# Layer 0 of a four-layer graph network: place 4 of a part hands on five far targets instead of four, and ScalarE scales three of them there

## The chip, the cores and the metric

The kernel runs on one core of a Trainium2 chip, in one launch. The core has a matrix engine (TensorE, PE in the profile; its weight loads are listed as PEld), a vector engine (VectorE, DVE), an engine for activation functions (ScalarE, ACT), a general engine (GpSimd, POOL) and a queue that issues transfers (SyncE, SP). Each works through its own list of instructions in order and waits for the others by semaphores. The metric is the device time of one execution in microseconds (us); before the change it is 3322.97 us, the median of three executions (3311.76 to 3326.16).

## What is computed

Four layers work on `x`, 64 graphs of 256 nodes with 256 features each, and on `adj`, 64 matrices of 256x256. The change is in layer 0 alone. That layer is a recurrence over the nodes: step `i` replaces row `i` of the state `h`, and the row is worked out from a weighted sum over all rows, among them those that earlier steps have replaced.

```python
def step(h, i):
    x = jnp.take(h_e, i, axis=1)
    row = jnp.take(norm_adjT, i, axis=1)
    x_par = jnp.einsum('bj,bjd->bd', row, h)
    iou = x @ W_ioux.T + b_ioux + x_par @ W_iouh.T + b_iouh
    r, z = jnp.split(iou, 2, axis=1)
    r, z = (jax.nn.sigmoid(r), jax.nn.sigmoid(z))
    hc = jnp.tanh(x @ W_coux.T + b_coux + x_par * r @ W_couh.T + b_couh)
    h_new = z * x_par + (1.0 - z) * hc
    h = jax.lax.dynamic_update_slice(h, h_new[:, None, :], (0, i, 0))
    return (h, None)
```

So there are 256 steps, each of which needs the one before. Layers 1 to 3 (two graph convolutions and two kinds of attention, each with a residual and a layer norm) follow; no line of them is touched.

## The kernel before

All of layer 0 is in `_recurrence`. A step works on one 128x128 tile: 64 graphs times two halves of the features on the 128 partitions, 128 features along them. The steps are grouped into parts of `U = 8`; the *place* of step `n` in its part is `p = n % 8`. The order of instructions on every engine is the order in which the program writes them (`tc.manual_schedule()`), so no scheduler moves anything.

The chain of a step is this. The sum `xp` (L878) is turned on TensorE (L612) and copied by ScalarE (`xpT`, L614). TensorE makes the gates from it (`h_part`, L605). ScalarE takes the sigmoid (`rs`, L836), TensorE turns it (L838), VectorE multiplies (`rT`, L840), TensorE makes the candidate (L605), ScalarE takes the tanh in place (L873, its tile is called `rc`). VectorE makes `zcc` (L875) and the next step's `xp` (L878). While that runs TensorE also adds the input's share for the next step (`x_part`, L597), and behind it stands the turn of the next `xp` (L612).

What a new state adds to the sums of later steps is spread over several engines. `sums[a]` (tile `ACC`) holds the sums of part `a`, and step `n` has state `j = n - 1` in hand. Its targets `m` are the steps from `n + 1` up to the end of the next part.

- The *near* targets go into the list `pushes` and are added by VectorE one at a time (L630, `ACC[m] += keep * S`). At places 1 to 7 the one for step `n + 1` comes first, then five more, and up to two more after the instruction that makes `v` (L865, its tile is called `keep`). What remains is added in the next step.
- The last `FAR[p]` targets are the *far* ones. They are remembered in `far` and dealt with in the next step, in one batch: `scale_far` lets ScalarE scale the first `begun` of them into the tile `far` (L667, directly behind `xpT` and ahead of `rs`), GpSimd scales the rest in one instruction (L672) and adds all of them to `ACC` in one (L676). The tile `far` has one buffer.
- GpSimd's list in a step is: `ready` (L817, the sum of step `n + 1` times its factor, which needs the first push), L672, L676, at places 3 and 4 the additions of `early_sb` (L830), at places 6 and 7 those of `late_sb` (L888). Now and then a piece of a table `An` (L479) or of a tile `xA` (L333) is cut at the end of a step, both from tiles that a transfer fills.

With `FAR = (3, 5, 5, 5, 4, 4, 3, 4)`, place 3 of part `a` hands on targets 8a+11 to 8a+15, and they are added at place 4. At place 4 the new state 8a+3 has eleven targets, 8a+5 to 8a+15: seven near ones, to 8a+11, and four far ones, 8a+12 to 8a+15, which are added at place 5. VectorE's list at place 4 is therefore: `keep` and `hs` (the state, L646 and L648), six pushes, `rT`, L858, `v` (L865), the seventh push (8a+11), `zcc`, `xp`.

SyncE issues the transfers: new states into a ring `Hw` (L656), from which at places 0 to 3 TensorE makes the `late` sums (L521), and loads and stores for the `early` sums, the tables and the sums `Us`.

Of the kernel before, what the change touches and what calls it, by code (L numbers as in the profile page):

```python
# [70 lines left out]
def _recurrence(tc, ident, Hd, x, adj, W_ioux, b_ioux, W_iouh, b_iouh, W_coux, b_coux, W_couh, b_couh, wide, then):  # L71
# [27 lines left out]
    XB = 4  # L99
    NG = B // 4  # L100
    HB = B // 2
    FAR = (3, 5, 5, 5, 4, 4, 3, 4)

    with ExitStack() as ctx:
        const = ctx.enter_context(tc.tile_pool(name="r_const", bufs=1))
# [140 lines left out]
        def next_of(queue, n):  # L246
            if queue:
                queue.pop(0)(n)
# [371 lines left out]
        def cell(j, m, count=1):  # L620

            a, u = divmod(m, U)
            k, i = divmod(m, T)
            return sums[a][:, u:u + count, :], tables[k]["S"][:, LAG + j - k * T, i:i + count]
# [37 lines left out]
        def scale_far(j, hs, first, count, begun):  # L662

            acc, s = cell(j, first, count)
            tmp = work.tile([P, 5, P], F32, tag="far", name=f"far_{j}_{first}", bufs=1)
            for e in range(begun):
                nc.scalar.activation(tmp[:, e, :], hs, AF.Copy, scale=s[:, e:e + 1])  # L667

            def finish():
                if begun < count:  # L670
                    shape = [P, count - begun, P]
                    nc.gpsimd.tensor_mul(  # L672
                        tmp[:, begun:count, :], hs.unsqueeze(1).to_broadcast(shape),
                        s[:, begun:count].unsqueeze(2).to_broadcast(shape),
                    )
                nc.gpsimd.tensor_add(acc, acc, tmp[:, 0:count, :])  # L676

            return finish
# [89 lines left out]
        for now in range(N):  # L768
            n = now
            k, i = divmod(n, T)  # L770
            p = n % U
# [1 line left out]

            xpT = flip(xp, "xpT", n)
            next_of(copies, n)
            add_far = far and scale_far(*far, min(2, far[-1]))

            far = []
            if n:
# [4 lines left out]
                to = list(range(n + 1, end))  # L784
                near = to[:len(to) - max(0, min(FAR[p], len(to) - 2))]
                far = (n - 1, hs, to[len(near)], len(to) - len(near)) if near != to else []
# [686 lines left out]
def kernel(ctx: ExitStack, tc: tile.TileContext, ins, out):  # L1473
# [14 lines left out]
    def load_layers(load):  # L1488
        weights.extend(
            _load_layers(nc, wide, load, ins["L1_gnn_W"], ins["L1_gnn_b"], l2, l3)  # L1490
        )

    _recurrence(
        tc, ident, Hd, x, adj,
        *(ins["L0_gnn_" + n] for n in (
# [44 lines left out]
```

## Time and profile before

| what | number |
|---|---|
| median of three executions | 3322.97 us (3311.76 to 3326.16) |
| the profiled execution: its time / the span of its instructions | 3317.71 us / 3315.6 us |
| layer 0's steps in the profiled execution | about 138 to 1475 us of the span |
| busy in 138 to 1475 us: PE / DVE / POOL / ACT | 1210.94 / 979.48 / 910.10 / 806.28 us |
| DMA engines' busy share in that stretch | 0.66 |
| one push, L630, 128x128 | 343 ns, 1592 of them |
| one scaling on ScalarE, L667, 128x128 | 397 ns, 503 of them |
| L672 on GpSimd, 128x128 / 128x256 / 128x384 | 399 / 613 / 826 ns |
| L676 on GpSimd, 128x384 / 128x512 / 128x640 | 1000 / 1273 / 1550 ns |
| `early_sb`'s addition L830, 128x512 | 1273 ns |
| usual length of a step at places 3, 4, 5, 6 (from the end of one `xp` to the next, median) | 4.89, 5.23, 5.11, 4.63 us |

The durations are means of groups of one shape between 200 and 1400 us, but for L630 and L667, which are given with their counts in the whole run. A time in a list of instructions counts from the start of the span. In square brackets behind an instruction stands how long its engine was idle before it, and which instruction let it go on. ACT's and DVE's instructions overlap with their neighbours a little, so that a row's length is more than what it adds to a queue: two scalings in a row are listed as 0.69 us together, not 0.79. The lengths of steps are medians over the 32 parts, read off the starts and ends of the instructions L878.

### The profile page before, as it was taken

To read this page: it belongs to the slowest core of one execution; us is meant where nothing else is said; L and a number is where in the kernel's file an instruction comes from. 1 tells how busy PE (TensorE), PEld (TensorE's weight loads), DVE (VectorE), ACT (ScalarE), POOL (GpSimd) and SP (SyncE) were. 2 spreads that over 40 slices of the span, in tenths; PEclk is the share of its full clock that TensorE was granted. 3 is DMA by queue.
4 is the path that set the end of the run, shared out by engine and by line. 5 is a ranking of instruction groups with operands and counts; after the bars stand their busy time and mean duration, and the time that the engine had idled before them with its cause. 6 is when DMAs were issued, how large, how long until landed. Compare 5 with 4: busy or idle time off the path is not lost.

```text
span 3315.6 us, 80692 instructions
## 1 busy us (share of the span) xinstructions
PE 3072.3 (93%) x28332; PEld 2274.1 (69%) x28332; DVE 2592.5 (78%) x7391; ACT 1982.0 (60%) x5193; POOL 1873.1 (56%) x2226
## 2 busy tenths in 40 slices
PE   5799998998888998976999999999999999999997
PEld 4566665555555555545888888888888888888885
DVE  3477777766666777765888888888888888888885
ACT  0266665655555665644666666666666666666664
POOL 2376776766566877843555555555555555555543
PEclk8999999999899999998999999999999999999998
DMA  9856676788777575334333333333333333333310
GB/s 300 244 163 157 170 196 153 179 195 210 188 192 168 150 186 146 100 77 94 76 77 79 77 77 79 79 77 75 80 76 79 77 78 77 78 77 77 77 43 20
DMA packets 807151, 398.35 MB, mean 120 GB/s; under 512 B 525148, under 2 KB 773096, under 8 KB 801512
## 3 DMA queue, kind: packets, MB, share of 16 engines
q1 hardware_dynamic: 789048, 376.25, 46.4%
q10 hardware_dynamic: 17696, 16.91, 1.5%
q8 instruction: 227, 3.72, 0.5%
q14 instruction: 180, 1.47, 0.1%
HBM read 274.34 MB, written 99.61 MB: 113 GB/s over the span
## 4 chain that ended last, share of the span: by engine, by line
PE 77%; DMA 8%; POOL 5%; DVE 4%; issue 3%; SPq 2%; ACT 1%; POOLq 0%; ACTq 0%; DVEq 0%
PE mm L1017 14%; PE rc L605 6%; PE rc L597 4%; PE s L1243 4%; PE mm_3v L1017 4%; PE mm_2f L1017 4%; PE late L521 3%; PE mm_2v L1017 3%; PE mm_3f L1017 3%; PE mm_t L1017 3%; PE mm_g L1017 3%; PE mm_2w L1017 3%; PE mm_2s L1017 3%; PE o L1278 3%; POOL ACC L676 2%
## 5 line engine op out<-in xcount | busy, mean ns | idle before, releaser
L1255 POOL TENSOR_TENSOR p3s<-p 128x256 f32<-128x256 f32 x512 | 358.7, 732 | 271.9 <-ACT p L1253 271.6
L1017 PE MATMUL mm<-xT,weights 128*128 128x256 f32 x2048 | 484.2, 385 | 2.7 <-ACT xT L1133 2.7
L630 DVE SCALAR_TENSOR_TENSOR ACC<-keep,S,ACC 128x128 f32<-128x128 f32 x1592 | 447.6, 343 | 39.3 <-POOL ACC L676 24.3
L676 POOL TENSOR_TENSOR ACC<-ACC,far 128x640 f32<-128x640 f32 (+2 forms) x312 | 404.3, 1296 | 69.5 <-ACT far L667 30.6
L1017 PEld LDWEIGHTS mm<-xT,weights 128*128 128x128 f32 x2048 | 386.4, 191 | 80.2 <-ACT xT L1133 28.8
L1252 DVE TENSOR_TENSOR p<-s,neg 128x512 f32<-128x512 f32 x512 | 317.7, 683 | 85.6 <-PE s L1243 85.6
L973 ACT ACTIVATE y<-y,shift,rstd 128x256 f32<-128x256 f32 x512 | 279.7, 596 | 158.1 <-DVE shift L971 157.9
L1253 ACT ACTIVATE p<-p 128x512 f32<-128x512 f32 x512 | 307.2, 629 | 3.5 <-DVE p L1252 3.0
L817 POOL TENSOR_TENSOR ready<-ACC,dinv 128x128 f32<-128x128 f32 x255 | 101.8, 399 | 312.1 <-DVE ACC L630 309.5
L597 PE MATMUL rc<-WxT,xqT 128*64 128x256 f32 x2048 | 275.7, 390 | 1.8 <-issue 1.8
L965 POOL TENSOR_TENSOR rstd<-rstd,mhalf 128x2 f32<-128x2 f32 x256 | 173.5, 696 | 134.9 <-DVE rstd L964 133.1
L672 POOL TENSOR_TENSOR far<-hs,S 128x384 f32<-128x384 f32 (+1 forms) x310 | 222.0, 716 | 4.7
L1292 DVE RECIPROCAL rT<-o 128x256 f32<-128x256 f32 x128 | 223.8, 1748 | 0.0
L961 DVE BATCH_NORM_STATS2 st<-y 128x6 f32<-128x256 f32 x512 | 209.6, 409 | 12.5 <-POOL y L1154 9.7
L605 PE MATMUL rc<-WhT,rT 128*64 128x128 f32 x2048 | 172.6, 290 | 37.3 <-DVE rT L840 33.6
L1165 ACT ACTIVATE qk<-mm,weights 128x256 f32<-128x256 f32 x256 | 107.3, 470 | 161.4 <-PE mm L1017 159.5
L521 PE MATMUL late<-Hw,An 64*32 64x256 f32 x3840 | 166.4, 400 | 40.3 <-DMA Hw<-hs 18.5
L1154 POOL TENSOR_TENSOR y<-y,g 128x512 f32<-128x512 f32 x64 | 81.1, 1267 | 215.3 <-ACT g L1151 179.3
L605 PEld LDWEIGHTS rc<-WhT,rT 128*64 128x64 f32 x2048 | 109.2, 138 | 133.9 <-DVE rT L840 110.9
L605 PE MATMUL rc<-WhT,xpT 128*64 128x128 f32 x2048 | 170.0, 287 | 17.6 <-ACT xpT L614 17.5
L614 ACT COPY xpT<-xpT_ps 128x128 f32<-128x128 f32 x256 | 68.0, 265 | 195.3 <-PE xpT_ps L612 195.0
L597 PEld LDWEIGHTS rc<-WxT,xqT 128*64 128x64 f32 x2048 | 140.6, 140 | 56.3 <-ACT rc L873 10.2
(169 smaller groups left out, 7375.0 us busy)
## 6 DMA issues: line engine op xcount, KB each, us to landing
xX<-in_x_dram ACTq DMA_DIRECT2D x16, 1024.0 KB
Us<-xu SPq DMA_DIRECT2D x64, 256.0 KB
xq<-in_x_dram SPq DMA_DIRECT2D x64, 256.0 KB
ACC<-Us SPq DMA_DIRECT2D x32, 512.0 KB
Es<-eu SPq DMA_DIRECT2D x64, 256.0 KB
early_sb<-Es SPq DMA_DIRECT2D x32, 512.0 KB
xin<-in_x_dram SPq DMA_DIRECT2D x64, 256.0 KB
ad<-in_adj_dram SPq DMA_DIRECT2D x64, 256.0 KB
```

The lines of the kernel that those rows point to most:

```text
L521: nc.tensor.matmul(pb[g][q * T:(q + 1) * T, e, :], An[rows, b].rearrange("p u s -> p (u s)"), Hw[rows, b, :], start=True, stop=True,)
L597: nc.tensor.matmul(G[o * B:(o + 1) * B], xqT[a, i // 2][:, i % 2, kc, h * B:(h + 1) * B], WxT[:, kc, o, gates], start=False, stop=False, s ...
L605: nc.tensor.matmul(G[o * B:(o + 1) * B], hT[:, kc * B:(kc + 1) * B], WhT[:, kc, o, g], start=False, stop=(kc == 1), skip_group_check=True,)
L630: nc.vector.scalar_tensor_tensor(acc[:, 0, :], keep[:, j % 2, :], s, acc[:, 0, :], ALU.mult, ALU.add)
L672: nc.gpsimd.tensor_mul(tmp[:, begun:count, :], hs.unsqueeze(1).to_broadcast(shape), s[:, begun:count].unsqueeze(2).to_broadcast(shape),)
L676: nc.gpsimd.tensor_add(acc, acc, tmp[:, 0:count, :])
L973: nc.scalar.activation(y[:, c, :], y[:, c, :], AF.Identity, bias=shift[:, c:c + 1], scale=rstd[:, c:c + 1],)
L1017: nc.tensor.matmul(pm[:, c, :], lhsT[:, k, c * P:(c + 1) * P], rhs[:, k, :], start=(k == 0), stop=(k == 1),)
L1252: nc.vector.tensor_add(p, s_ps[i], self.neg3)
L1253: nc.scalar.activation(p, p, AF.Exp, scale=ISQ)
L1255: nc.gpsimd.tensor_add(both, p[:, 0, :], p[:, 1, :])
L1292: nc.vector.reciprocal(rT, o_ps[:, 1, :])
```

## The change

```diff
-    FAR = (3, 5, 5, 5, 4, 4, 3, 4)
+    FAR = (3, 5, 5, 5, 5, 4, 3, 4)
...
-            add_far = far and scale_far(*far, min(2, far[-1]))
+            add_far = far and scale_far(*far, min(3 if p == 4 else 2, far[-1]))
```

`FAR[4]` goes from four to five. Target 8a+11 of state 8a+3 is no longer VectorE's seventh push at place 4; it is one of a batch of five (8a+11 to 8a+15) that is scaled and added at place 5. The second line works at place 4 on the batch that place 3 handed on: ScalarE scales three of those five, and GpSimd two.

The lists of the engines change as follows, in 31 of the 32 parts (in the last part fewer targets are left, and nothing changes).

| engine, place | before | after |
|---|---|---|
| DVE, place 4 | six pushes, then one behind `v` | six pushes, none behind `v` |
| ACT, place 4 | two scalings between `xpT` and `rs` | three |
| POOL, place 4 | L672 128x384, L676 128x640 | L672 128x256, L676 128x640 |
| POOL, place 5 | L672 128x256, L676 128x512 | L672 128x384, L676 128x640 |

The counts of instructions on PE, ACT, POOL and SP by kind are otherwise as before, apart from the 31 pushes that VectorE loses and the 31 scalings that ScalarE gains; no transfer is added, removed or moved in its queue.

## The prediction

> **What bounds the kernel now.** I read the page's costliest groups first, then VectorE's waits in layer 0, then one step at place 4 in order of time on each engine. Two groups of the page carry the work that the change shifts:
>
> ```profile
> L630 DVE SCALAR_TENSOR_TENSOR ACC<-keep,S,ACC 128x128 f32<-128x128 f32 x1592 | 447.6, 343 | 39.3 <-POOL ACC L676 24.3
> L676 POOL TENSOR_TENSOR ACC<-ACC,far 128x640 f32<-128x640 f32 (+2 forms) x312 | 404.3, 1296 | 69.5 <-ACT far L667 30.6
> ```
>
> The end of the first line matters: before pushes VectorE sat idle for 39.3 us, 24.3 of them until a far addition on GpSimd was done. VectorE's waits between 140 and 1475 us (who waits for whom, us in total, times, longest) say in how many places:
>
> ```profile
> DVE zcc L875 <- ACT rc L873: 123.0, 132, 7.1
> DVE ACC L630 <- POOL ACC L676: 24.3, 30, 1.2
> DVE keep L865 <- POOL ready L817: 13.2, 2, 8.7
> ```
>
> Thirty times, about once a part. Where it is shows in order of time. VectorE in step 100 (place 4 of part 12):
>
> ```profile
> 647.87 0.36 DVE L865 SCALAR_TENSOR_TENSOR keep<-keep,Sd,ready 128x128 f32<-128x128 f32 x1
> 648.99 0.35 DVE L630 SCALAR_TENSOR_TENSOR ACC<-keep,S,ACC 128x128 f32<-128x128 f32 x1 [0.76 <-POOL ACC L676]
> 649.26 0.28 DVE L875 TENSOR_TENSOR zcc<-zc,rc 128x128 f32<-128x128 f32 x1
> 649.57 0.35 DVE L878 SCALAR_TENSOR_TENSOR xp<-zcc,Sd,keep 128x128 f32<-128x128 f32 x1
> ```
>
> GpSimd in the same step:
>
> ```profile
> 646.15 0.40 POOL L817 TENSOR_TENSOR ready<-ACC,dinv 128x128 f32<-128x128 f32 x1 [0.85 <-DVE ACC L630]
> 646.51 0.83 POOL L672 TENSOR_TENSOR far<-hs,S 128x384 f32<-128x384 f32 x1
> 647.41 1.54 POOL L676 TENSOR_TENSOR ACC<-ACC,far 128x640 f32<-128x640 f32 x1
> 648.91 1.27 POOL L830 TENSOR_TENSOR ACC<-ACC,early_sb 128x512 f32<-128x512 f32 x1
> ```
>
> And ScalarE:
>
> ```profile
> 645.27 0.69 ACT L667 ACTIVATE far<-hs,S 128x128 f32<-128x128 f32 x2
> 646.34 0.28 ACT L836 ACTIVATE rs<-rc 128x128 f32<-128x128 f32 x1 [0.37 <-PE rc L605]
> 648.38 0.26 ACT L873 ACTIVATE rc<-rc 128x128 f32<-128x128 f32 x1 [0.31 <-PE rc L605]
> ```
>
> The seventh push writes target 8a+11. GpSimd's addition from 647.41 covers 8a+11 to 8a+15 and stands ahead of that push in the program, so the push waits until 648.99. The tanh had ended at 648.64. `zcc` could have followed it directly; it starts at 649.26, since it stands behind the push. Its sum is not read before step 8a+11, seven steps later, yet it holds up the recurrence. At other places pushes that stand behind `v` (place 3, for one) write targets which the running addition doesn't cover, and no row shows them waiting.
>
> How much of that the chain feels is read on TensorE. From tanh's start to the next turn of `xp` (L612) it is 1.60 us here (648.38 to 649.98). Two steps later, where nothing waits:
>
> ```profile
> 658.71 0.26 ACT L873 ACTIVATE rc<-rc 128x128 f32<-128x128 f32 x1 [0.43 <-PE rc L605]
> ...
> 659.84 0.33 PE L612 MATMUL xpT_ps<-ident,xp 128*128 128x128 f32 x1
> ```
>
> That is 1.13 us, and TensorE has no gap there, as it comes straight from `x_part`. So 0.47 us of the 0.59 us by which `zcc` is late is lost; the next 0.12 us would be covered by `x_part`.
>
> [...] For prices I use the trace[...], and L676 goes from 1273 to 1550 ns; [...] and the second scaling adds 0.69 less 0.40, or 0.29 us.
>
> **The change, part by part.** *The push goes (31 times).* I formed the time from tanh's start to the next L612, less 1.124 us (the finer value of 1.13), at place 4 of each of the first 31 parts: 17 parts show 0.47 or 0.48 us (sum 8.07), four 0.37 to 0.43 (1.56), two 0.58 (1.15), five 0.83 to 0.95 (parts 7, 25, 27, 28 and 29, where GpSimd comes late from two additions of early sums or a cut; 4.62), one 0.12, and two nothing. Sum 15.5 us. The push's own 0.34 us is in that sum and gives nothing more. What is late next is TensorE's `x_part`; it is why I take 15.5 us and not the 24.3 us of the waits.
>
> *The third scaling on ScalarE (31 times 0.29 us).* It stands between `xpT` and `rs`, which is on the chain. `rs` starts 0.37 us after the second scaling ends, waiting for TensorE; as instructions may overlap by 0.11 us, 0.48 us are free. I read the same room in each part: 0.47 us or more in 16 of 31, 0.33 to 0.34 in the others, against 0.29 needed. TensorE hides it everywhere, in those 15 parts with 0.04 us to spare only. Cost 0; if that cover failed it would be 31 x 0.29 = 9.1 us at most, less where `rT` waits for VectorE's pushes anyway.
>
> *GpSimd at place 4.* L672 is 0.21 us shorter (826 to 613 ns). It lets L676 and L830 end earlier by that. Now nothing on the chain waits for L676, so no gain.
>
> *GpSimd at place 5.* L672 takes 0.21 and L676 0.28 us more, together 0.49 us. L676 now covers 8a+11, so it must wait for the sixth push of place 5: in part 12 the scaling would be done about 0.1 us before that push is, a wait of some 0.1 us. Behind it stand `ready` of place 6 (L817) and, through the one buffer of `far`, ScalarE's scalings at place 6. Before `ready` at place 6 GpSimd idles 1.0 us or more in 28 of 31 parts, and in the other three `ready` ends 1.9 us or more before L865 starts. Cost 0; bound 31 x 0.6 = 18.6 us if no cover existed.
>
> *`ready` at place 5.* The steps come earlier by up to 0.95 us, GpSimd's list of place 4 by 0.21 only. The tightest parts (22, 25, 26, 28, 29) have 0.52, 0.87, 0.52, 0.84 and 0.84 us between the end of `ready` and L865; each keeps 0.1 to 0.15 us. Cost 0, bound 0.2 us each.
>
> *Waits on transfers.* In 14 parts place 0 is longer than its usual 4.70 us by 0.9 to 6.6 us, 46 us in all, as TensorE's late sums wait for `Hw` and other transfers; in parts 13 and 17 `ready` at place 5 waits behind a cut that waits for `raw` (4.5 and 8.7 us). SyncE's queue works there without a pause from place 4 on, so a step that arrives earlier can just wait longer. Gains ahead of such a wait: 5.6 us before the long places 0, 0.9 in parts 13 and 17, 1.0 before waits in parts 24 and 27: 7.5 us at risk. The trace can't show how much is swallowed. Bounds: 0 and 7.5 us, and below nothing (waits that shrink) as executions differ by 14 us anyway. I take 3 us, less than half, because part of those transfers wait themselves for states or sums that come earlier too.
>
> Sum: 15.5 - 3 = 12.5 us; the profiled execution's 3317.7 us becomes 3305.2. The median lies 5.3 us above that execution, which gives 3310.5; I say 3310.
>
> **The rivals.** *Kept in full.* Transfers follow the steps and their waits shrink a little: 3323 - 15.5 - 4 = 3303. For it: late parts (27 to 30, 3.2 us) have hardly a transfer wait, and SyncE waited often for VectorE. Against: the busy DMA share of 0.66.
> *Swallowed.* All 7.5 us are lost, and `rs` or `ready` take some 3 us more: gain 5 us, 3318. For it: long unbroken stretches of SyncE's queue between 490 and 512 us. Against: the parts without such waits hold 8 us by themselves.
> *Slower: `ready` behind the transfer of `raw`.* Place: place 4 or 5 of parts with a cut L479. GpSimd stands in order; when `raw` isn't there, `ready`, `v` and all else wait, which cost 3.6 and 7.9 us beyond a usual step twice in this trace. If earlier steps shift the queue so that four more parts are caught at 6 us each, and the transfers swallow half the gain, it is 3323 + 24 - 8 = 3339. It decides from three such parts on (18 us against the 15.5). Against: the change adds no transfer.
>
> **How the numbers follow.** Forecast (3310) 0.45, kept in full 0.28, swallowed 0.17, slower 0.10. A measurement of this kernel can tell about 0.5%, 16.6 us, from no change. Faster by more than that, below 3306.4: the rival kept in full nearly whole (0.26) and the lower two fifths of the forecast (0.18), 0.44. Slower by more than that, over 3339.6: some half of the last rival and a little spread, 0.06. The rest, 0.50, is within. Range 3297 to 3326: down to the full gain with its spread of 6 us, up past the swallowed case with executions' spread; it leaves out the slower rival and small tails.
>
> **What would show it.** In the changed trace VectorE's wait for L676 (24.3 us, 30 times) should be gone, `zcc` at place 4 start about 0.03 us behind the tanh's end, and place 4 be shorter by about 0.5 us. `rs` at place 4 should still wait for TensorE. L676 at place 5 should show a short wait for VectorE's push. I am wrong if `rs` is released by a scaling, if `ready` at place 5 or 6 ends L865's waits in many parts, or if places 0 to 3 grow by what place 4 loses.

## The result, and the profile after

| | before | after |
|---|---|---|
| median of nine executions | 3317.74 us (3311.76 to 3326.16) | 3307.10 us (3298.50 to 3317.09) |
| the profiled execution: time / span | 3317.71 / 3315.6 us | 3312.54 / 3310.8 us |
| before the first turn L612 / all steps / behind the last turn | 136.17 / 1336.41 / 1843.03 us | 140.53 / 1326.65 / 1843.63 us |

The ratio of after to before is 0.9964 [0.9947, 0.9982] (it is not the quotient of the medians, which is 0.9968); the medians lie 10.6 us apart. Nine executions put the kernel before at 3317.74 us; the 3322.97 that the prediction started from were the first three of them. Forecast were 3310 us, by a gain of 12.5. The gain is under the 0.5% (16.6 us) that the prediction took to be the least one could tell from no change; with nine executions of each the interval nevertheless ends below 1.

The span fell by 4.8 us only. The steps themselves took 9.8 us less, and 4.4 us came on before the first step, where no line of the change is at work. A single execution of each says little about the total: between two profiles of the changed kernel place 0 alone differs by 8.7 us (227.7 below and 236.4 when it was run again). Where time moved is therefore read from the rows of a place, and how much it is worth from the medians.

VectorE's waits between 140 and 1475 us, after (who waits for whom, us in total, times, longest):

```profile
DVE zcc L875 <- ACT rc L873: 138.6, 164, 7.8
...
DVE ACC L630 <- POOL ACC L888: 16.4, 7, 4.0
DVE keep L865 <- POOL ready L817: 14.2, 2, 9.7
```

The line of the pushes with L676, 24.3 us in 30 waits before, is gone. `zcc` waits for the tanh 164 times instead of 132, which is as it should be, since the tanh is on the chain and the push was not. L888's 16.4 us were 10.3 in four waits before; GpSimd's addition of `late_sb`, for which they wait, waits for a transfer itself. The two waits for `ready` are the same two parts as before. The page's groups say the same (31 pushes fewer, L630's idle time 20.8 us instead of 39.3, of which 16.4 behind L888):

```profile
L630 DVE SCALAR_TENSOR_TENSOR ACC<-keep,S,ACC 128x128 f32<-128x128 f32 x1561 | 436.8, 343 | 20.8 <-POOL ACC L888 16.4
L676 POOL TENSOR_TENSOR ACC<-ACC,far 128x640 f32<-128x640 f32 (+2 forms) x312 | 412.8, 1323 | 67.5 <-ACT far L667 27.6
```

In order of time, VectorE in step 100 (place 4 of part 12), after:

```profile
650.92 0.36 DVE L865 SCALAR_TENSOR_TENSOR keep<-keep,Sd,ready 128x128 f32<-128x128 f32 x1
651.73 0.29 DVE L875 TENSOR_TENSOR zcc<-zc,rc 128x128 f32<-128x128 f32 x1 [0.45 <-ACT rc L873]
652.05 0.35 DVE L878 SCALAR_TENSOR_TENSOR xp<-zcc,Sd,keep 128x128 f32<-128x128 f32 x1
```

ScalarE in the same step:

```profile
648.32 0.98 ACT L667 ACTIVATE far<-hs,S 128x128 f32<-128x128 f32 x3
649.38 0.28 ACT L836 ACTIVATE rs<-rc 128x128 f32<-128x128 f32 x1
...
651.43 0.26 ACT L873 ACTIVATE rc<-rc 128x128 f32<-128x128 f32 x1 [0.31 <-PE rc L605]
```

The tanh ends at 651.69 and `zcc` starts at 651.73; before it started 0.62 us after the tanh's end. The three scalings are listed as 0.98 us, 0.29 more than two, and `rs` starts 0.08 us after they end (649.30 to 649.38), where before it started 0.37 us after the second; a gap under 0.15 us gets no bracket in these lists. So `rs` is still released by TensorE here, with less room. GpSimd at places 4 and 5:

```profile
649.56 0.61 POOL L672 TENSOR_TENSOR far<-hs,S 128x256 f32<-128x256 f32 x1
650.25 1.54 POOL L676 TENSOR_TENSOR ACC<-ACC,far 128x640 f32<-128x640 f32 x1
...
653.75 0.83 POOL L672 TENSOR_TENSOR far<-hs,S 128x384 f32<-128x384 f32 x1
654.77 1.55 POOL L676 TENSOR_TENSOR ACC<-ACC,far 128x640 f32<-128x640 f32 x1 [0.20 <-DVE ACC L630]
```

The bracket in the last row is the wait for the sixth push that was forecast for place 5, at 0.20 us instead of 0.1. Nobody is late by it.

The steps by place, each from one start of L612 to the next and summed over all parts (us, one profiled execution each):

| place | 0 | 1 | 2 | 3 | 4 | 5 | 6 | 7 |
|---|---|---|---|---|---|---|---|---|
| before | 225.7 | 154.7 | 152.0 | 155.5 | 165.1 | 172.9 | 154.1 | 156.4 |
| after | 227.7 | 155.1 | 149.8 | 154.6 | 149.4 | 175.2 | 155.4 | 159.4 |

Place 4 lost 15.7 us; the other places together gained 5.9. Among them are the places with waits on transfers (us, times, longest). Before:

```profile
PE late L521 <- DMA Hw<-hs: 18.5, 6, 4.9
POOL ACC L888 <- DMA late_sb<-Lb: 14.1, 6, 5.9
```

After:

```profile
PE late L521 <- DMA Hw<-hs: 23.7, 8, 4.8
POOL ACC L888 <- DMA late_sb<-Lb: 21.5, 8, 5.9
```

Two more waits of each kind, with nearly the same longest: it looks as if the steps come earlier and the transfers don't.

Over all steps the clock is no part of the difference between these two profiles. The trace lists the clock that TensorE was granted, and it is at half in some stretches of layer 0: for 71.7 us of the steps before and 71.8 after.

### The profile page after: what moved, and what is told of

It reads as the page before. It is cut to its first block, busy times and chain, and to the rows that moved or that the text cites. A ratio compares the mean times of both kernels' runs of the same rounds, so it can differ in the third digit from the quotient of the medians.

```text
span 3310.8 us, 80661 instructions
## 1 busy us (share of the span) xinstructions
PE 3074.5 (93%) x28332; PEld 2276.0 (69%) x28332; DVE 2587.2 (78%) x7360; ACT 1991.1 (60%) x5224; POOL 1881.3 (57%) x2226
## 4 chain that ended last, share of the span: by engine, by line
PE 77%; DMA 8%; DVE 7%; SPq 3%; issue 2%; POOL 2%; ACT 1%; ACTq 0%; DVEq 0%; POOLq 0%
PE mm L1017 14%; PE rc L605 6%; PE rc L597 4%; PE s L1243 4%; PE mm_2f L1017 4%; PE mm_3v L1017 4%; PE late L521 3%; PE mm_2v L1017 3%; PE mm_3f L1017 3%; PE mm_t L1017 3%; PE mm_g L1017 3%; PE mm_2w L1017 3%; PE mm_2s L1017 3%; PE o L1278 3%; DVE ACC L630 3%
## 5 line engine op out<-in xcount | busy, mean ns | idle before, releaser
L630 DVE SCALAR_TENSOR_TENSOR ACC<-keep,S,ACC 128x128 f32<-128x128 f32 x1561 | 436.8, 343 | 20.8 <-POOL ACC L888 16.4
L676 POOL TENSOR_TENSOR ACC<-ACC,far 128x640 f32<-128x640 f32 (+2 forms) x312 | 412.8, 1323 | 67.5 <-ACT far L667 27.6
L672 POOL TENSOR_TENSOR far<-hs,S 128x384 f32<-128x384 f32 (+1 forms) x310 | 222.0, 716 | 4.7
L521 PE MATMUL late<-Hw,An 64*32 64x256 f32 x3840 | 167.2, 400 | 41.2 <-DMA Hw<-hs 23.7
L605 PE MATMUL rc<-WhT,xpT 128*64 128x128 f32 x2048 | 169.9, 287 | 17.6 <-ACT xpT L614 17.6
L667 ACT ACTIVATE far<-hs,S 128x128 f32<-128x128 f32 x534 | 183.7, 397 | 3.2 <-POOL ACC L676 1.3
L875 DVE TENSOR_TENSOR zcc<-zc,rc 128x128 f32<-128x128 f32 x256 | 73.2, 286 | 138.7 <-ACT rc L873 138.6
```

What stands on the lines that cost most here:

```text
L521: nc.tensor.matmul(pb[g][q * T:(q + 1) * T, e, :], An[rows, b].rearrange("p u s -> p (u s)"), Hw[rows, b, :], start=True, stop=True,)
L605: nc.tensor.matmul(G[o * B:(o + 1) * B], hT[:, kc * B:(kc + 1) * B], WhT[:, kc, o, g], start=False, stop=(kc == 1), skip_group_check=True,)
L630: nc.vector.scalar_tensor_tensor(acc[:, 0, :], keep[:, j % 2, :], s, acc[:, 0, :], ALU.mult, ALU.add)
L672: nc.gpsimd.tensor_mul(tmp[:, begun:count, :], hs.unsqueeze(1).to_broadcast(shape), s[:, begun:count].unsqueeze(2).to_broadcast(shape),)
```

## The experiments

Each ratio is to the kernel before in the runs beside it. "Place 4" is the sum over all parts as in the table above.

| run | ratio | median, this / before (us) | place 4 (us) |
|---|---|---|---|
| change again | 0.9972 [0.9959, 0.9984] | 3307.94 / 3316.62 | 150.6 |
| push one place later | 0.9981 [0.9972, 0.9989] | 3309.21 / 3316.61 | 150.2 |
| five far, two scaled | 0.9985 [0.9974, 0.9995] | 3310.44 / 3316.61 | 150.2 |
| four far, three scaled | 0.9983 [0.9970, 0.9997] | 3312.90 / 3316.61 | 160.4 |
| one idle push | 0.9964 [0.9951, 0.9976] | 3305.34 / 3316.62 | 152.2 |
| three idle pushes | 0.9996 [0.9982, 1.0010] | 3310.63 / 3312.75 | 168.8 |
| six idle pushes | 1.0058 [1.0038, 1.0077] | 3333.76 / 3316.61 | 201.9 |
| degrees moved | 0.9982 [0.9974, 0.9991] | 3309.47 / 3316.62 | 148.6 |
| push later, degrees moved | 0.9972 [0.9963, 0.9981] | 3307.36 / 3316.62 | 149.5 |
| changed, ring early | 1.0060 [1.0038, 1.0081] | 3332.58 / 3312.75 | 152.2 |
| before, ring early | 1.0044 [1.0024, 1.0064] | 3329.60 / 3312.75 | 165.2 |
| changed, ring from place 5 | 0.9987 [0.9975, 0.9999] | 3312.89 / 3315.69 | 149.1 |

**Push one place later.** The kernel before, in which the seventh push of place 4 only moves to place 5, where it is the sixth push, ahead of `rT` and not, as the expectation says, behind `v`; the last push of place 5 then stands behind `v`. Every engine does the work it did.

```diff
-                push(2)
+                push(0 if p == 4 and n < N - U else 2)
```

> The kernel before, with the seventh push of place 4 kept on VectorE but given out one place later, behind v of place 5, where nothing has to be waited for. VectorE's, ScalarE's and GpSimd's work stays as it was before the change. If the gain of the change is the wait at place 4 (theory), this kernel gains what the change gained: ratio to before 0.996, some 12 us, and in its profile the time from turn to turn at place 4 falls by 15 to 16 us in sum and the waits for the far addition are gone. If the gain is that VectorE has 31 pushes less to do (31 x 0.34 = 10.6 us), it gains nothing: ratio 1.000. If it comes from the batches on ScalarE and GpSimd, also nothing.

VectorE's waits, push one place later:

```profile
DVE zcc L875 <- ACT rc L873: 123.5, 151, 7.7
...
DVE keep L865 <- POOL ready L817: 15.2, 7, 9.4
...
DVE ACC L630 <- POOL ACC L888: 10.7, 5, 4.5
```

The wait for L676 is gone and place 4 falls to 150.2 us with no push saved and nothing handed to GpSimd. So what paid at place 4 is the order: the push is no longer in front of `zcc`. Place 5, which takes over the push, keeps its usual 5.22 us; its sum is 9.4 us larger than before in this profile, nearly all of it in parts 3, 7, 17 and 19. The median is 7.4 us lower, where 12 were expected. The second row has seven waits where before and after have two. The five new ones are parts 22, 25, 26, 28 and 29 at place 5, just those that the prediction had listed as the tightest for `ready`; there L865 starts 0.24 to 0.33 us behind its forerunner instead of the usual 0.10, some 0.9 us in sum. In the changed kernel `ready` in those parts ends 48 to 149 ns before L865 starts; where L865 waits for it, that distance is 34 ns.

**Five far, two scaled**: the diff's first line alone.

```diff
-    FAR = (3, 5, 5, 5, 4, 4, 3, 4)
+    FAR = (3, 5, 5, 5, 5, 4, 3, 4)
```

> The first line of the change alone: five far targets at place 4, ScalarE scales two at every place. Theory: the wait is gone, and the third scaling buys nothing on the chain: ratio to before 0.996 as for the whole change, within 2 us of it; GpSimd ends place 4 later by 0.21 us, so ready at place 5 becomes late in parts 22, 26, 28 and 29 by up to 0.2 us each, under 1 us in sum. Rival: the third scaling carries part of the gain: then 3 us or more of it are missing here.

Place 4 is down to 150.2 us again, and `ready` shows the same seven waits (12.6 us). The first line brings the gain (the median is 6.2 us lower, where some 12 were expected). What the third scaling adds on top is the relief of GpSimd by 0.21 us, which removes those five small waits; the medians (3310.44 against 3307.94 us of the change run again) lie that way, but the intervals overlap, and of the difference only those waits, 0.8 us in sum, are seen in a trace.

**Four far, three scaled**: the diff's second line alone.

```diff
-            add_far = far and scale_far(*far, min(2, far[-1]))
+            add_far = far and scale_far(*far, min(3 if p == 4 else 2, far[-1]))
```

> The second line alone: four far targets at place 4, ScalarE scales three at place 4. Theory: the push at place 4 still waits for the far addition, which ends 0.21 us earlier as GpSimd scales one target less; place 4 falls by 0.21 us in some 29 parts, 6 us in sum, and with a fifth to a third given back to transfers 4 to 5 us remain: ratio 0.9985. Rival, that the scaling alone buys the gain: 0.996. Rival, that the third scaling delays the sigmoid: 1.000 or more.

VectorE's wait, four far, three scaled:

```profile
DVE ACC L630 <- POOL ACC L676: 18.7, 30, 1.1
```

Still 30 waits, each shorter by 0.19 us (24.3 less 18.7, over 30): GpSimd's addition comes earlier by its shorter scaling, and the push behind it as well. Place 4 fell by 4.7 us and the total by 3.7. The two lines of the diff overlap: either shortens the same wait, so their gains can't be added.

**One, three and six idle pushes.** The changed kernel with pushes put back behind `v` at place 4. They read and write what nothing else uses at that time, so they wait for nobody.

```diff
                 push(2)
+                for _ in range(3 if p == 4 and n < N - U else 0):
+                    nc.vector.scalar_tensor_tensor(
+                        xp, keep[:, (n - 1) % 2, :], cell(n - 1, n + 7)[1], xp, ALU.mult, ALU.add
+                    )
```

(One or six in the place of three in the other two.)

> The changed kernel with one push behind v at place 4 that waits for nothing and whose result isn't used: VectorE's list at place 4 is again as long as before the change. If only the wait mattered, the push fits between v and the tanh's end (0.45 us of idle time, 0.35 us of push): place 4's sum stays at 149 to 150 us and the time is that of the changed kernel within 2 us. If VectorE's work was what the change saved, place 4 grows back by up to 31 x 0.34 = 10.6 us.

One push keeps the whole gain: the ratio is that of the change. Place 4's sum is 152.2 us, somewhat over the 149 to 150 expected, but 2.5 us of that are in part 18, whose place 4 is long and uneven in every profile; the usual length is 4.75 us as after the change. The work of 31 pushes is worth nothing at this spot, where VectorE is idle; that they waited cost the time. "It is the fewer pushes" falls with this run.

> The changed kernel with three idle pushes behind v at place 4, which lengthen place 4 by about as much as the wait of the kernel before did. If they wait for each other (0.38 us each, as six of them showed: 52 us in sum), zcc comes 0.7 us later, 0.12 of it covered: place 4's sum is about 168 us, against 165 before the change. If the gain is place 4's time and nothing else, the total is back at the level of the kernel before, ratio 0.999 to 1.002. If the change gains by something else as well (less work on VectorE, other batches), the ratio stays under 0.999.

VectorE in step 100, three idle pushes (these added lines shift `zcc` to L879 and `xp` to L882):

```profile
647.00 0.36 DVE L865 SCALAR_TENSOR_TENSOR keep<-keep,Sd,ready 128x128 f32<-128x128 f32 x1
647.39 1.12 DVE L868 SCALAR_TENSOR_TENSOR xp<-keep,S,xp 128x128 f32<-128x128 f32 x3
648.43 0.28 DVE L879 TENSOR_TENSOR zcc<-zc,rc 128x128 f32<-128x128 f32 x1
```

`zcc` again follows a push without a gap, and place 4 takes 5.27 us in most parts, where before it took 5.23 and after takes 4.75. Nothing is left of the gain that could be told from none (0.9996 [0.9982, 1.0010]). Late by about the same amount, `zcc` costs about the same, whatever makes it late.

> The changed kernel with six pushes more behind v at place 4, into a tile that is overwritten right after, so that they delay the chain by a known time: zcc starts 1.1 us later if they overlap as other pushes do, 1.9 us later if each waits for the one before; 0.12 us of that is covered by TensorE. So place 4 grows by 32 to 54 us in sum over 31 parts. It measures how much of a time at place 4 reaches the end: if waits on transfers swallow a third of it, the total grows by two thirds of what place 4 grows; if they swallow nothing, by all of it. The forecast took a fifth (3 of 15.5 us).

Six pushes raise place 4 by 52.5 us over the changed kernel (201.9 less 149.4), and the median by 26 us (33.76 less 7.94 above 3300, 25.8 by the change run again): about half arrives. In this run's profiled execution (3354.24 us, the slowest of its six) the steps took 45 us longer than after the change. Place 4 grew by 52.5 us and place 5 by 23.5 (198.7), while places 0 and 7 shrank by 18.3 and 8.9 (209.4 and 150.5). The growth of place 5 goes with TensorE's clock: in this profile it is at half for 63.7 us of place 5, against 5.5 after the change. TensorE in step 37 (place 5 of part 4), six idle pushes:

```profile
331.28 0.33 PE L612 MATMUL xpT_ps<-ident,xp 128*128 128x128 f32 x1 [1.60 <-DVE xp L878]
...
332.69 1.12 PE L605 MATMUL rc<-WhT,xpT 128*64 128x128 f32 x8
```

The same step after the change:

```profile
324.25 0.33 PE L612 MATMUL xpT_ps<-ident,xp 128*128 128x128 f32 x1
...
325.65 0.66 PE L605 MATMUL rc<-WhT,xpT 128*64 128x128 f32 x8
```

The step took 8.32 us instead of 5.21, and the granted clock in it was 0.59 instead of 1.00. Why it fell there isn't shown; in this step TensorE had idled for 1.60 us just before. So two things act against each other in this run, time that places 0 and 7 take up and time that the lower clock adds, and the medians' "half" is not a measure of the first alone.

**The change again**, beside the later runs.

> The changed kernel once more, beside the others on one chip. Place 4 should again fall by 15 to 16 us in sum in its profile. If half of that is given back to transfers, as the kernel with six idle pushes showed in the other direction, the ratio to before is 0.9975; if the forecast's fifth is right, 0.9962; if the first measurement (0.9964) was right it is repeated within 0.001.

0.9972, nearest to the first of the three: 8.7 us by the medians, where the first comparison gave 10.6. Place 4 is at 150.6 us, 14.5 less than before. In this profile (3316.09 us, the slowest of its ten executions) the other places together are 11.3 us longer than before, 10.7 of them at place 0.

**Degrees moved.** In each block of 32 steps VectorE works out the degrees for the next block in 14 pieces, each written at the end of a step and so ahead of the next step's pushes; three of them stand ahead of place 4. Three of the 14 are moved one step on, which takes two away from place 4. This was tried on the changed kernel, and on the kernel with the push one place later.

```diff
-                if i in (0, 2, 3, 8, 10, 11, 12, 15, 16, 17, 19, 20, 22, 24):
+                if i in (0, 2, 4, 8, 10, 12, 13, 15, 16, 17, 19, 20, 22, 24):
```

> The changed kernel with the sums of degrees that stand at the end of place 3 (steps 3 and 11 of a table's 32) moved to the end of place 4, where VectorE idles 0.83 us before rT. With the seventh push gone, place 4 is 4.66 us where such a sum stands ahead of it and 4.29 us where none does, so 14 parts should lose 0.37 us: place 4's sum falls by 5 us, place 5's stays. With half given back 2.5 us remain, under 0.1%. Rival: the sums now make place 5 late, and nothing is gained.

> The kernel before with both orders changed and no work moved between engines: the seventh push of place 4 given out at place 5, and the sums of degrees at steps 3 and 11 moved to steps 4 and 12. Place 4 should be about 145 us in sum, 20 us under before; with half given back the ratio is 0.997. Rival: at place 5 the moved sum, six pushes and the one behind v are too much for VectorE, or ready comes late behind them, and place 5 grows by what place 4 loses.

On the changed kernel place 4 fell by 0.8 us against the change's own profile, and the total did not improve (0.9982). Of the parts that lost their piece two went from 4.76 us at place 4 to the 4.38 of parts without one, and most of the others to 4.63 only: TensorE's early sums are next there. Part 18 took back 0.8 us, in a place 4 that is long in every profile. On the other kernel place 4 is at 149.5 us, not the 145 expected, and the ratio is 0.9972 instead of 0.9981, with overlapping intervals. Neither beats the change.

**Ring early.** SyncE sends new states to `Hw` at places 4 to 7 only, two a step, so that those of places 0 to 3 gather. If the lost part of the gain is lost to that queue, sending all at once should bring it back. Tried on both kernels, and a third time with two at place 4 and all that are left at place 5.

```diff
-                    for _ in range(min(2, len(ring_in))):
+                    for _ in range(len(ring_in)):
```

> The changed kernel with new states sent to the ring Hw as soon as places 4 to 7 allow it: all five that wait at place 4, then one a step, instead of two a step. Nothing else in SyncE's queue changes but that order. If place 0 is late because the last states of a part reach the ring late behind other transfers, the last one stands further ahead in the queue, place 0's sum (226 to 236 us) falls by 5 us or more, and the kernel beats the changed one (3308). Rival, that the transfer engines are simply full there: place 0 stays as it is, within the spread of 5 us that single profiles show.

> The kernel before with the same earlier sending of states to the ring. Beside the changed kernel in the same form it gives the worth of the change where the ring comes sooner. If the waits for the ring are what takes back 5 to 7 of the 15.5 us, the pair lies 11 us or more apart; if the waits come from full transfer engines, the pair lies 8 to 10 us apart as the kernels do without it.

> The changed kernel that sends two states to the ring at place 4 as before and all that wait from place 5 on, so that late_sb's transfer keeps its place in SyncE's queue, unlike in the kernel that sent five at place 4 (place 0 fell by 36 us there and place 7 rose by 45, waiting for late_sb). If only the order of these two transfers made place 7 late, place 7 stays at 155 to 160 us, place 0 falls by 10 us or more from 228 to 236, and the ratio to before is 0.994. Rival, that the transfer engines have no room for the earlier ones: what place 0 gains, places 5 to 7 lose, and the ratio is 0.997 or more.

Waits on transfers, changed kernel with the ring early:

```profile
POOL ACC L888 <- DMA late_sb<-Lb: 67.5, 25, 10.0
...
PE late L521 <- DMA Hw<-hs: 3.0, 3, 1.6
```

The sends did come earlier: TensorE's wait for `Hw` fell from 23.7 to 3.0 us and place 0 from 227.7 to 191.5. But in the program's order the load of `late_sb` (L507) now stands behind the sends of all five states that wait at place 4, ten transfers instead of four, and GpSimd's wait for it rose from 21.5 to 67.5 us; VectorE's pushes wait behind that addition (55.5 us), and place 7 takes 204.0 us instead of 159.4. Both kernels lost by it (1.0060 and 1.0044), and beside each other the change gained nothing at all: 3332.58 against 3329.60 us. Place 4 still gives its 13.0 us; place 7 takes 9.7 of them and place 0 another 4.3. The expectation that the pair would lie 8 us or more apart was wrong: all of the gain is given back here. In this pair the clock differs too, at half for 93.6 us of the steps in the changed kernel and 75.1 in the other, about half of it at place 7 in both, so the waits need not be the whole of it.

With that load's place kept (ring from place 5) place 0 is 224.0, place 7 160.1 us, and the ratio 0.9987 no better than the change's. The forecast 10 us at place 0 came only against the second profile of the changed kernel (236.4), not against the first (227.7). So the queue's order decides which place waits, and neither new order makes the kernel faster. Whether the limit is the issuing of transfers or the moving of the bytes stays open.

## Why the prediction was right

*The push goes: 15.5 us at place 4.* The profile after has 15.7 less, the second one 14.5. It also holds part by part: in 26 of the 31 parts place 4 fell within 0.02 us of what the prediction had read for that part. That the sum was formed from tanh's start to the next L612, and not from the 24.3 us of waits, is what made it right: TensorE's `x_part` covers the rest. The runs with one and with three idle pushes show it is the start of `zcc` which counts, and the push one place later that no work had to go for it.

*The third scaling: 0.* Right, by as little as was said. In all but two parts `rs` at place 4 starts as long after the end of `xpT` as before (0.82 or 0.96 us); in 15 parts 0.04 us of room are left, in nearly all others 0.19. The sign given for it was only half right: `rs` was to "still wait for TensorE", but in the 15 parts ScalarE goes from the third scaling to `rs` with no idle time at all, and in the others the idle time is mostly 0.08 us, as in the step shown.

*GpSimd at place 5: 0, with 0.1 us of wait for the sixth push.* The wait is 0.20 us; no cost, as `ready` of place 6 has its reserve.

*`ready` at place 5: 0, with 0.1 to 0.15 us of room in five parts.* The room was smaller than said: `ready` ends 48 to 149 ns before L865 starts, of which 34 ns pass even where L865 waits for it, and in the second profile part 22 has 35 ns, that is nothing left. It cost nothing, by luck of some hundredths of a microsecond. The runs without the third scaling show what the room was worth: the same five parts wait 0.13 to 0.22 us each with the push one place later.

*Waits on transfers: 3 us given back of 7.5 at risk.* The term was too small. Medians give 10.6 and 8.7 us of the 15.7 and 14.5 that place 4 lost, so 5 to 6 are given back; the profile's other places grew by 5.9. It lies within the bounds of 0 to 7.5 us which the prediction had set. Parts 28 and 29, which wait for no transfer in the profiles before and after, keep the gain whole: place 4 from 5.33 to 4.38 us, the remaining seven steps 32.65 us in both. In the second profile part 28 does wait for `Hw`, and its remaining steps take 36.0 us. The profiles before and after place the loss at places 0, 5, 6 and 7, with two more waits each for `Hw` and `late_sb`; the second places nearly all of it at place 0. That the waits on transfers are the cause is likely, and the ring-early pair supports it, but it isn't shown: no run takes those waits away. Which transfer swallowed which 5 us can't be read from single executions that differ by as much.

*The rivals.* "Kept in full" was 19.5 us less, "swallowed" 5 us less. The two comparisons give 6.0 to 17.6 us (0.9982 and 0.9947 of 3317.74) and 5.3 to 13.6 us (0.9984 and 0.9959 of 3316.62); both rivals lie outside, "swallowed" only just, and the forecast's 12.5 inside of both. "Slower" needed further parts in which `ready` at place 5 stands behind a cut; they are the same two, 13 and 17, with 8.90 and 14.04 us at place 5 after and 8.85 and 13.08 before. The rival had no part in the result.

One part was chance. The forecast's 3310 came from 12.5 us off 3322.97, and the kernel before is 5 us quicker by nine executions; the gain was 2 to 4 us smaller, and the two errors partly cancelled.

## What to carry to other kernels

Look in each engine's list for work that isn't due yet but stands, with a wait of its own, ahead of an instruction of the recurrence: at that place moving it behind was worth the same as removing it (150.2 against 149.4 and 150.6 us). Price it by what the chain's next instruction comes earlier, not by the wait in the list, and then ask how much of it is lost in later steps, to waits on transfers that don't come earlier above all; in this kernel a third or more was lost, and with transfers running later everything. Before work is moved to an engine that looks idle, count the room that the following instructions have there in every part, since 0.04 us was enough for `rs`, and in the runs without the third scaling the five parts in which `ready` had none left waited.

## What was not expected of the hardware

L558 makes a 128x32 tile on VectorE from two inputs, eight times in the kernel. In part 27 of the change run again it took 1.25 us (GpSimd, which was adding `early_sb`, and VectorE, from one list by time):

```profile
1313.36 2.62 POOL L830 TENSOR_TENSOR ACC<-ACC,early_sb 128x512 f32<-128x512 f32 x2
1313.43 1.25 DVE L558 TENSOR_TENSOR Sd<-S,dinv 128x32 f32<-128x32 f32 x1
```

With the push one place later, the same part:

```profile
1303.03 1.55 POOL L676 TENSOR_TENSOR ACC<-ACC,far 128x640 f32<-128x640 f32 x1
...
1304.39 0.24 DVE L558 TENSOR_TENSOR Sd<-S,dinv 128x32 f32<-128x32 f32 x1
1304.54 2.63 POOL L830 TENSOR_TENSOR ACC<-ACC,early_sb 128x512 f32<-128x512 f32 x2
```

In the first, GpSimd had begun an addition of 1.27 us 0.07 us before L558, and L558 lasted until 0.05 us after the end of that addition. In the second, L676 was running when L558 started and ended 0.19 us later, and L558 again ended 0.05 us after it. This holds throughout: in the 14 profiles of this case L558 starts 88 times while an instruction of GpSimd runs, and in 85 of them it ends 45 to 54 ns after that instruction does (in the other three GpSimd was within 0.07 us of its end); the 24 times that none ran it took 197 to 210 ns. What holds L558 back isn't shown, only when it ends. Part 27's L558 took 0.39 us before the change, where it started 0.92 us after GpSimd's addition (L830) had begun, and 1.24 after it, where it started 0.08 us after; the longer hold costs some 0.56 us in that step of the changed kernel (place 5, 5.23 us instead of 4.67). So a shift of 0.84 us between the two engines' lists decided this step.

VectorE's pushes into different rows start 0.26 us apart (six in 1.64 us), and the idle pushes, which all add into the same tile, 0.385 us apart (three in 1.12 us): in this row, in which each push needs the one before it, a push took nearly half as much time again.
